# A graph network's edge loop: w1 rows asked for earlier, three smaller last node blocks, and fewer groups copied by hand

## The chip, the cores and the metric

The kernel runs on one core of a Trainium2 chip. The core has five engines that run their own queues of instructions in order: TensorE (PE; its weight loads are shown as PEld), VectorE (DVE), ScalarE (ACT), GpSimd (POOL) and SyncE (SP, which here only issues transfers). The metric is the device time of one execution in microseconds; of several timed runs the median counts.

## What is computed

One layer of a gated graph network over 12500 nodes and 400000 edges, everything in float32. Edges are sorted by their destination `dst`; the source `src` of an edge is any node. With `h = relu(layernorm(x))`:

```python
h = jnp.concatenate([x[s], x[d], ea], axis=-1)          # x is h here; 128 + 128 + 32 columns
m = jax.nn.relu(h @ w1 + b1) @ w2 + b2
agg = jax.ops.segment_sum(m, d, num_segments=x.shape[0])
gi = agg @ w_ih + b_ih
gh = x @ w_hh + b_hh
...
r = jax.nn.sigmoid(i_r + h_r)
z = jax.nn.sigmoid(i_z + h_z)
n = jnp.tanh(i_n + r * h_n)
return (1.0 - z) * n + z * x
```

The result is added to the layer's input. The last four lines are the node update; what stands above `gi` is the edge work.

## The kernel before

**Tables first.** A short first stage normalises all nodes, keeps `h` transposed in the core's memory (`hT_all`, 128 features by 12500 nodes) and writes the table A = h @ w1[0:128] to main memory. A second table, B = h @ w1[128:256] + b1, is made in batches of 512 nodes during the edge loop (`batch_product`, `batch_store`, 32 groups ahead of their use, AHEAD). So the first product of an edge is A[src] + B[dst] + ea @ w1[256:288].

**Groups and units.** The edges come in 391 groups of 1024 (8 tiles of 128 edges), each group in two units of four tiles, 782 units in all. Since edges are sorted by destination, a group touches few nodes: two windows of 32 rows of B, eight nodes apart, hold all destinations of a group.

**One unit.** `stages(u)` writes down work for several units ahead, and `other(phase)` sprinkles the rest between. For a unit:
- `fetch(q)` loads tile L for two groups: destinations repeated over 64 partitions (L533) and the transposed edge features (L536), two transfers of 256 KB on SP's queue. L has three buffers, so the load of L number q waits until TensorE has read number q - 3.
- `onehot_T` on VectorE turns the destinations in L into a one-hot matrix (L545).
- `window_rows(k)` loads the B rows of the group's two windows into RW, beside the w1 rows of the edge features (L575, two transfers of 16 KB). RW has four buffers, taken in turn by k mod 4. Since B lives in main memory, the load waits for the store of its batch.
- `pre(u)` on TensorE multiplies L by RW (L644): this gives B[dst] + ea @ w1 for the unit's four tiles in one bank.
- The A[src] part comes in one of two ways. For most groups, `gather(k)` has POOL issue eight indirect transfers, one for each tile of 128 rows of A (L152), into G, a ring of 12 buffers; VectorE adds G to the product and applies the relu in one instruction (`add`, L668). For "hand groups" nothing is gathered: ScalarE or VectorE copies the 1024 needed columns of `hT_all` one by one (`one_by_one`; ScalarE one column at a time, L905; VectorE two at a time, L912, unpacked by L917), TensorE multiplies them by w1 (L655), and ScalarE applies the relu (`relu`, L675). SPREAD says how many hand groups each engine has; `run_jobs` spreads the copying of one evenly over the units since the one before. The last hand groups are 382 (VectorE) and 385 (ScalarE).
- `seg(u)` on TensorE sums the edges' rows onto the windows' 64 places with another one-hot matrix (L683, L688), and `take(k)` copies the sums out after each group (L696).

The first ten groups are gathered from x itself and normalised in place, since A is not ready by then.

**Order.** Every engine runs its queue as the program writes it. `gathers(u)` writes the gathers of a group down as soon as the buffer's last reader has been written; POOL's queue holds nearly nothing else, so it runs ahead until a buffer is missing. SP's queue holds all loads and stores, `fetch`, `window_rows`, the stores of B and of the output, and stands still at the first one that must wait. `window_rows(k + 3)` is written in the second unit of group k, in phase 2; `pre` of group k's first unit is written three units before it, in `stages`.

**Nodes.** Nodes are updated in blocks of up to 14 groups (512 nodes). BLOCKS lists each block's first group, its groups and its width. When the loop reaches the next block's first group, `node(b)` starts: it sums the block's windows (`sum_of`, L713), carries the overlap over (`carry`, L724, L727), makes the four gates on TensorE, applies sigmoid and tanh on ScalarE, combines on VectorE and stores the rows. It yields some 13 times, and one step is taken at the end of each unit. LEAST bounds the distance of two blocks' first nodes; NW counts the blocks of full width. ROOM enters a check that no window needs rows of B that are not stored yet; if a check of that kind fails, a slow general path recomputes all, which did not run here.

**The last block** has a function of its own, `last_node`, whose steps are taken in the units LAST_STEPS. Its eight groups' sums are added one by one as they come, and its gates start before the last sum is there. Two of its steps, the gate matmuls (L830, L833), are taken after the loop, between the last `seg` and the last `take`'s `sum_of`.

Of the kernel before, what the change touches and what calls it, by code (L numbers as in the profile page):

```python
# [9 lines left out]
F32 = mybir.dt.float32  # L10
# [17 lines left out]
NU = 2 * NP  # L28

V = 32  # L30
# [2 lines left out]

BP, BW = 14, 512
DMIN = 320
BLOCKS = [(BP * b, BP, BW) for b in range(27)] + [(378, 5, 256), (383, 8, 320)]
NB = len(BLOCKS)
NW = 27
LEAST = [DMIN] * 28 + [16]
QP = 2  # L40
W = 96
NT = -(-N // 128)
# [3 lines left out]
GBUFS = 12  # L46
BATCH = 512
AHEAD = 32
ROOM = V * (AHEAD - 2)
PLACE = 20  # L50
CH = PLACE * PAIR
LOAD = {"act": 16, "dve": 32}
PIECE = 128
STEP = {"act": 4, "dve": 8}
SPREAD = {"dve": 26, "act": 24}
START = {"dve": 16, "act": 4}
NR = 12672

# [4 lines left out]
def tile_gnn(ctx: ExitStack, tc: tile.TileContext, x, src, srcT, dstT, dstP, eaT, eaP, w1, b1, w2T, b2,  # L63
# [11 lines left out]
    ps2 = ctx.enter_context(tc.tile_pool(name="ps2", bufs=2, space=bass.MemoryType.PSUM))  # L75
# [662 lines left out]
    def node(b):  # L738
        w = BLOCKS[b][2]
        g0, xb, offs = block_start(b)  # L740
        pt = ps1.tile([128, 512], F32, name="nd")[:, :w]
        pd = ps1.tile([128, 512], F32, name="misc")[:, :w]
        nc.vector.tensor_copy(dcol[:2 * V, :len(offs)], sums[:, :len(offs), D])
        zero(pt)
        for i in range(len(offs)):
            sum_of(b, pt, offs, i)
        zero(pd)
        for i in range(len(offs)):
            degree_of(b, pd, offs, i)
        d = step_of(b)  # L750
        yield 1
        carry(b, TOT, pt, d)
        carry(b, DEG[0:1, :], pd[0:1, :], d)
        yield 1
        g = nc.tensor.value_load(blk_i[0:1, b:b + 1], min_val=0, max_val=N - w)
        hT = hT_all[:, bass.ds(g, w)]

        def gate(name, i, with_h, with_s):
            c = slice(i * D, (i + 1) * D)
            ci = slice(2 * D, 3 * D) if i == 3 else c  # L760
            pg = ps1.tile([128, 512], F32, name=name)[:, :w]
            nc.tensor.matmul(pg, brow[:, c], DEG[:, :w], start=True, stop=False)  # L762
            if with_h:
                nc.tensor.matmul(pg, whh_s[:, ci], hT, start=False, stop=not with_s)
            if with_s:
                nc.tensor.matmul(pg, w2ih[:, ci], TOT[:, :w], start=False, stop=True)  # L766
            return pg

        pr = gate("nd", 0, True, True)
        yield 1  # L770
        r = temp(w)
        nc.scalar.activation(r, pr, AF.Sigmoid)  # L772
        ph = gate("misc", 3, True, False)
        yield 1
        t = temp(w)
        nc.vector.tensor_tensor(t, r, ph, op=ALU.mult)
        pi = gate("nd", 2, False, True)
        yield 1
        nc.vector.tensor_tensor(t, t, pi, op=ALU.add)
        pz = gate("misc", 1, True, True)  # L780
        yield 1
        nc.scalar.activation(t, t, AF.Tanh)
        z = temp(w)
        nc.scalar.activation(z, pz, AF.Sigmoid)
        yield 1
        gv = nc.vector.value_load(blk_i[0:1, b:b + 1], min_val=0, max_val=N - w)
        q = r
        nc.vector.tensor_tensor(q, hT_all[:, bass.ds(gv, w)], t, op=ALU.subtract)
        yield 1
        nc.vector.tensor_tensor(q, q, z, op=ALU.mult)  # L790
        yield 1
        nc.vector.tensor_tensor(q, q, t, op=ALU.add)
        yield 1
        po = ps1.tile([128, 512], F32, name="nd")[:w // 4, :]
        for i in range(4):
            nc.tensor.transpose(po[:, i * D:(i + 1) * D], q[:, i::4], ident)
        yield 1
        nc.vector.tensor_tensor(xb, xb, po.rearrange("p (i f) -> p i f", i=4), op=ALU.add)
        yield 4 if b < NW - 1 else 1
        nc.sync.dma_start(out[bass.ds(g0, w), :].rearrange("(p i) f -> p i f", i=4), xb)  # L800

    def last_node():
        b = NB - 1
        k0, n, w = BLOCKS[b]
        g0, xb, offs = block_start(b)
        yield
        pd = wide[1][:, :w]
        zero(pd)
        for i in range(n):
            degree_of(b, pd, offs, i)  # L810
        d = step_of(b)
        g = nc.tensor.value_load(blk_i[0:1, b:b + 1], min_val=0, max_val=N - w)
        hT = hT_all[:, bass.ds(g, w)]
        gv = nc.vector.value_load(blk_i[0:1, b:b + 1], min_val=0, max_val=N - w)
        h = hT_all[:, bass.ds(gv, w)]
        pt = wide[0][:, :w]
        zero(pt)
        for i in range(n - 4):
            sum_of(b, pt, offs, i)
        yield  # L820
        carry(b, DEG[0:1, :], pd[0:1, :], d)
        for i in range(n - 4, n - 1):
            yield
            sum_of(b, pt, offs, i)
        yield

        def gate(pool, name, i, h_too):
            c = slice(i * D, (i + 1) * D)
            pg = pool.tile([128, 512], F32, name=name)[:, :w]
            nc.tensor.matmul(pg, brow[:, c], DEG[:, :w], start=True, stop=False)  # L830
            if h_too:
                ci = slice(2 * D, 3 * D) if i == 3 else c
                nc.tensor.matmul(pg, whh_s[:, ci], hT, start=False, stop=i == 3)  # L833
            return pg

        def finish(pg, i):
            nc.tensor.matmul(pg, w2ih[:, i * D:(i + 1) * D], TOT[:, :w], start=False, stop=True)

        pr = gate(ps1, "nd", 0, True)
        ph = gate(ps1, "misc", 3, True)  # L840
        yield
        pi = gate(ps2, "seg", 2, False)
        pz = gate(ps2, "pre", 1, True)
        yield
        sum_of(b, pt, offs, n - 1)
        carry(b, TOT, pt, d)
        finish(pr, 0)
        finish(pi, 2)
        finish(pz, 1)
        r, t, z = temp(w), temp(w), temp(w)  # L850
        nc.scalar.activation(r, pr, AF.Sigmoid)
        nc.vector.tensor_tensor(t, r, ph, op=ALU.mult)
        nc.vector.tensor_tensor(t, t, pi, op=ALU.add)
        nc.scalar.activation(z, pz, AF.Sigmoid)
        nc.scalar.activation(t, t, AF.Tanh)
        nc.scalar.activation(r, pz, AF.Sigmoid, scale=-1.0)
        nc.vector.tensor_tensor(z, z, h, op=ALU.mult)
        nc.vector.tensor_tensor(t, t, r, op=ALU.mult)  # L858
        nc.vector.tensor_tensor(t, t, z, op=ALU.add)  # L859
        po = ps1.tile([128, 512], F32, name="nd")[:w // 4, :]  # L860
        for i in range(4):
            nc.tensor.transpose(po[:, i * D:(i + 1) * D], t[:, i::4], ident)  # L862
        nc.vector.tensor_tensor(xb, xb, po.rearrange("p (i f) -> p i f", i=4), op=ALU.add)  # L863
        nc.sync.dma_start(out[bass.ds(g0, w), :].rearrange("(p i) f -> p i f", i=4), xb)
# [93 lines left out]
    gathers(0)  # L958
    for q in range(3):
        fetch(q)  # L960
    for k in range(3):
        window_rows(k)


# [30 lines left out]
                    left.pop(0)  # L995

    last = last_node()
    LAST_STEPS = (NU - 8, NU - 6, NU - 5, NU - 4, NU - 2, NU - 1)

    for u in range(NU):  # L1000
        k, h = divmod(u, 2)
        gathers(u)
        if h == 0:
            if k % QP == 0:
                fetch(k // QP + 3)
            if k and k == BLOCKS[block(k)][0]:
                nodes_left.append([node(block(k) - 1), 2 if k < BLOCKS[-1][0] else 1])
            if k % PLACE == 1:
                indices(k // PLACE + 2)
            if k % PLACE == 5:  # L1010
                place(k // PLACE + 1)
                dst_tile(k // PLACE + 2)
            if k == NP - 20:
                check_windows()
        if u == min(START.values()) - 2:
            nc.vector.tensor_scalar(at[:NJ, :], at[:NJ, :], 4.0, float(H_AT), op0=ALU.mult, op1=ALU.add)

        def other(phase):
            run_jobs(u, phase)
            if h == 0 and phase == 1 and batch_due(k):  # L1020
                batch_product(batch_due(k), wide[1], p3, "xb", 2)
            if h == 1 and phase == 1 and batch_due(k):
                batch_store(batch_due(k))
            if h == 1 and phase == 2:
                window_rows(k + 3)
            if h == 0 and phase == 3:
                take(k - 1)
            if phase == 3:
                step(nodes_left)
                if u in LAST_STEPS:  # L1030
                    next(last)

        other(0)
        stages(u)
        other(1)
        other(2)
        seg(u)
        if u == 0:
            node_setup()
        other(3)  # L1040
    for it, _ in nodes_left:
        run(it)
    next(last)
    next(last)
    take(NP - 1)
    run(last)

# [168 lines left out]
```

## Time and profile before

| | before |
|---|---|
| median of 3 timed runs | 3548.33 us (3529.08 to 3559.73) |
| the profiled execution, whole | 3567.68 us |
| its span, first to last instruction | 3565.9 us |
| granted clock of TensorE in it, mean | 0.783 |
| matmuls for RW by L (L644) | 3128, of 495 ns, busy 1149.9 us |
| segment sums (L688) | 6250, of 319 ns, busy 592.3 us |
| matmuls of hand groups (L655) | 416 of VectorE's groups, 384 of ScalarE's |
| transfers on POOL's queue | 178.76 MB, 21.5% of 16 engines' span |
| transfers on SP's queue | 153.56 MB, 15.8% |

A row of the profile's costliest groups gives line, engine, operation, tiles written and read, shapes and count, then the engine's busy time in it and the mean duration of one in ns, then the time the engine sat idle just before them and what ended most of that. Instructions of one engine overlap, so count times mean can be more than the busy time. A row of the waits says who waited for whom: microseconds in total, how many times, and the longest. "Issue" is time in which an engine waited for nothing that the profile shows. A row of the timeline begins with its start and length in us. SP's rows there are the issue of a transfer, not the transfer.

### The profile page before, as it was taken

The page shows a single profiled execution, that of the slowest core. Times are in us where ns is not written, and L with a number is a line of the kernel's source. Part 1 is how long each engine was busy: PE and PEld are TensorE (multiplying, and loading weights), DVE is VectorE, ACT ScalarE, POOL GpSimd, SP SyncE. Part 2 cuts the span into 40 slices and gives each one's busy share as a digit, 9 for nine tenths or more (in the row PEclk, how much of TensorE's full clock was granted, in tenths as well). Part 3 has the DMA queues.
Part 4 walks back from the last instruction along what each step waited for, and adds up shares of the span by engine and source line. Part 5 has one row for each costly group of instructions (what it writes and reads, how often), then busy time and mean ns, then how long its engine had stood idle before and what let it go on. Part 6 is the DMA issues. An engine that isn't in the chain of part 4 may idle for free. (4 is left out here: it accounts for less than half of the span.)

```text
span 3565.9 us, 80442 instructions
## 1 busy us (share of the span) xinstructions
PE 2409.1 (68%) x13224; PEld 1536.2 (43%) x13224; DVE 2266.0 (64%) x16484; ACT 2661.4 (75%) x25007; POOL 2614.4 (73%) x2734
## 2 busy tenths in 40 slices
PE   6567666675776676577667766765766676667768
PEld 6444444443444444344444443443444344434435
DVE  7656666666656666666566666666666666666664
ACT  5497778768777778787678688768876887796782
POOL 7677777777777777777777777777777777777770
PEclk8788877777777877777777878778777788787868
DMA  6433333333333333333333333333333333333431
GB/s 198 100 87 93 93 94 93 90 96 93 92 89 93 92 92 95 93 96 92 94 94 96 92 95 95 93 93 96 95 91 95 94 98 96 96 91 91 95 94 31
DMA packets 188489, 337.57 MB, mean 95 GB/s; under 512 B 65118, under 2 KB 108701, under 8 KB 187967
## 3 DMA queue, kind: packets, MB, share of 16 engines
q0 software_dynamic: 87200, 178.76, 21.5%
q1 hardware_dynamic: 100623, 153.56, 15.8%
q14 instruction: 412, 3.38, 0.3%
q8 instruction: 110, 1.80, 0.2%
q10 hardware_dynamic: 144, 0.07, 0.0%
HBM read 311.87 MB, written 20.27 MB: 93 GB/s over the span
## 5 line engine op out<-in xcount | busy, mean ns | idle before, releaser
L152 POOL DMA_INDIRECT G<-A,src_i x2648 | 2540.1, 959 | 839.6 <-issue 761.9
L905 ACT COPY HE_act<-hT_all 128x4 uint8 x24576 | 2470.3, 189 | 57.9 <-issue 38.3
L644 PE MATMUL pre<-RW,L 128*128 128x256 f32 x3128 | 1149.9, 495 | 1079.9 <-DMA RW<-B 827.5
L912 DVE SCALAR_TENSOR_TENSOR both<-hT_all 128x4 uint16 x13312 | 1138.0, 153 | 970.6 <-issue 961.4
L644 PEld LDWEIGHTS pre<-RW,L 128*128 128x128 f32 x3128 | 672.9, 240 | 1379.5 <-issue 669.8
L688 PE MATMUL seg<-RB,OH 128*32 128x129 f32 x6250 | 592.3, 319 | 0.0
L668 DVE CUSTOM_DVE_ANT_0 RB<-pre,G 128x512 f32<-128x512 f32 x662 | 448.5, 677 | 133.3 <-PE pre L644 98.8
L675 ACT ACTIVATE RB<-pre 128x512 f32<-128x512 f32 x120 | 70.7, 589 | 481.6 <-PE pre L655 481.3
L688 PEld LDWEIGHTS seg<-RB,OH 128*32 128x32 f32 x6250 | 326.8, 123 | 208.5 <-issue 159.0
L545 DVE TENSOR_SCALAR L<-L,node_of 64x512 f32<-64x512 int32 x383 | 187.2, 489 | 6.1 <-DMA L<-in_dstP 5.9
L772 ACT ACTIVATE gt<-nd 128x512 f32<-128x512 f32 (+1 forms) x28 | 16.5, 588 | 228.8 <-PE nd L766 228.8
L596 DVE TENSOR_TENSOR OH<-dloc,wide 128x256 f32<-128x256 f16 (+1 forms) x392 | 158.9, 406 | 0.5 <-issue 0.3
L696 DVE COPY sums<-seg 64x129 f32<-64x129 f32 x391 | 108.1, 277 | 17.2 <-PE seg L688 17.2
L683 PEld LDWEIGHTS <-zrow 1*64 1x64 bf16 x391 | 41.4, 106 | 143.4 <-issue 134.8
L683 PE MATMUL seg<-zrow 1*64 1x129 bf16 x391 | 99.4, 254 | 2.3 <-DVE sums L696 2.2
L917 DVE COPY HE_dve<-both 128x512 uint8<-128x512 uint8 x208 | 93.2, 448 | 7.1
L713 PE MATMUL nd<-spot,sums 64*128 64x40 f32 x766 | 94.2, 285 | 0.0
L713 PEld LDWEIGHTS nd<-spot,sums 64*128 64x128 f32 x766 | 90.7, 193 | 6.2 <-issue 6.1
L152 POOL DMA_INDIRECT G<-in_x,src_i x77 | 72.8, 945 | 24.4 <-issue 23.2
L655 PEld LDWEIGHTS pre<-w1a,HE_dve 128*128 128x128 f32 x416 | 75.6, 226 | 9.1
L655 PEld LDWEIGHTS pre<-w1a,HE_act 128*128 128x128 f32 x384 | 73.7, 239 | 9.1
L762 PE MATMUL nd<-DEG,brow 34*128 34x512 f32 (+1 forms) x112 | 75.0, 755 | 0.9 <-DVE DEG L727 0.9
(193 smaller groups left out, 1414.3 us busy)
## 6 DMA issues: line engine op xcount, KB each, us to landing
L<-in_dstP SPq DMA_DIRECT2D x195, 256.0 KB
L<-in_eaP SPq DMA_DIRECT2D x195, 256.0 KB
G<-A,src_i POOLq DMA_INDIRECT x2648
RW<-B SPq DMA_DIRECT2D x782, 16.0 KB
xb<-in_x SPq DMA_DIRECT2D x27, 256.0 KB
out<-xb SPq DMA_DIRECT2D x27, 256.0 KB
xs<-in_x SPq DMA_DIRECT2D x11, 512.0 KB
A<-asb SPq DMA_DIRECT2D x11, 512.0 KB
```

Of the source, the lines that this page charges most:

```text
L152: nc.gpsimd.indirect_dma_start(out=G[k][:, j, a, :], out_offset=None, in_=table, in_offset=bass.IndirectOffsetOnAxis(ap=src_i[c][:, i:i + ...
L545: nc.vector.tensor_scalar(o, i, node_of[:, k:k + 1], None, op0=ALU.is_equal)
L596: nc.vector.tensor_tensor(o, d.to_broadcast(shape), i.to_broadcast(shape), op=ALU.is_equal)
L644: nc.tensor.matmul(PP[u][:, 2 * i:2 * i + 2, :], Ls[k // QP][:, c0:c0 + 128], RW[k % 4], start=True, stop=not raw)
L655: nc.tensor.matmul(PP[u][:, 2 * i + a, :], cols, w1a, start=False, stop=n + 1 == len(l) or l[n + 1][1] != j)
L668: nc.vector._custom_dve(TENSOR_ADD_SAT, out=RB[u % 4][:, :, :D], in0=PP.pop(u), in1=unit(u), s0=float("inf"), s1=0.0)
L683: nc.tensor.matmul(SEG[k][:2 * V, :D + 1], zrow[:, :2 * V], zrow[:, :D + 1], start=True, stop=False)
L688: nc.tensor.matmul(SEG[k][V * a:V * (a + 1), :D + 1], OH[k][:, j, a, :], RB[u % 4][:, (j % 2) * 2 + a, :D + 1], start=False, stop=all(b != ...
L696: nc.vector.tensor_copy(sums[:, slot(block(k), k - BLOCKS[block(k)][0]), :], pm[:2 * V, :D + 1])
L713: nc.tensor.matmul(p[:, bass.ds(offs[i], V + SHIFT)], sums[:, slot(b, i), :D], spot, start=False, stop=i == len(offs) - 1)
L905: nc.scalar.copy(he[:, e * 4:e * 4 + 4], column(v))
L912: nc.vector.scalar_tensor_tensor(both[:, (e0 % PIECE + i) // 2, :], column(vals[i + 1]), 256.0, column(vals[i]), op0=ALU.mult, op1=ALU.add)
```

## The change

`window_rows` is asked for group k + 4 at the start of group k's first unit, ahead of that unit's `fetch`, and no more for k + 3 in the second unit. Four groups are asked for ahead of the loop. ROOM goes down to fit. SPREAD takes VectorE from 26 hand groups to 25 and ScalarE from 24 to 15. The last three node blocks are 10, 9 and 8 groups (before: 14, 5 and 8, behind one full block more), and `last_node` makes three of its gates in units of the loop, one each, with a step in unit NU - 3 that was not there; the z gate goes into the bank that held the degrees. After the loop `take` follows at once.

```diff
-BLOCKS = [(BP * b, BP, BW) for b in range(27)] + [(378, 5, 256), (383, 8, 320)]
+BLOCKS = [(BP * b, BP, BW) for b in range(26)] + [(364, 10, 384), (374, 9, 352), (383, 8, 320)]
-NW = 27
-LEAST = [DMIN] * 28 + [16]
+NW = 26
+LEAST = [DMIN] * 27 + [256, 128]
...
-ROOM = V * (AHEAD - 2)
+ROOM = V * (AHEAD - 4)
...
-SPREAD = {"dve": 26, "act": 24}
+SPREAD = {"dve": 25, "act": 15}
...
-        yield 4 if b < NW - 1 else 1
+        yield 4 if b < NW else 1
...
         carry(b, DEG[0:1, :], pd[0:1, :], d)
-        for i in range(n - 4, n - 1):
-            yield
-            sum_of(b, pt, offs, i)
         yield
...
-        pr = gate(ps1, "nd", 0, True)
-        ph = gate(ps1, "misc", 3, True)
+        sum_of(b, pt, offs, n - 4)
+        pz = gate(pd, 1, True)
         yield
-        pi = gate(ps2, "seg", 2, False)
-        pz = gate(ps2, "pre", 1, True)
+        pr = gate(bank(ps1, "nd"), 0, True)
+        yield
+        sum_of(b, pt, offs, n - 3)
+        ph = gate(bank(ps1, "misc"), 3, True)
+        yield
+        sum_of(b, pt, offs, n - 2)
+        pi = gate(bank(ps2, "pre"), 2, False)
         yield
         sum_of(b, pt, offs, n - 1)
...
-    for k in range(3):
+    for k in range(4):
         window_rows(k)
...
-    LAST_STEPS = (NU - 8, NU - 6, NU - 5, NU - 4, NU - 2, NU - 1)
+    LAST_STEPS = (NU - 8, NU - 6, NU - 5, NU - 4, NU - 3, NU - 2, NU - 1)
...
         if h == 0:
+            window_rows(k + 4)
             if k % QP == 0:
                 fetch(k // QP + 3)
...
-            if h == 1 and phase == 2:
-                window_rows(k + 3)
...
-    next(last)
-    next(last)
     take(NP - 1)
     run(last)
```

More of the change, by code (lines that the diff above doesn't have):

```diff
@@ L821, in last_node, with gate @@
         carry(b, DEG[0:1, :], pd[0:1, :], d)
-        for i in range(n - 4, n - 1):
-            yield
-            sum_of(b, pt, offs, i)
         yield
-        def gate(pool, name, i, h_too):
+        def gate(pg, i, h_too):
             c = slice(i * D, (i + 1) * D)
-            pg = pool.tile([128, 512], F32, name=name)[:, :w]
             nc.tensor.matmul(pg, brow[:, c], DEG[:, :w], start=True, stop=False)
@@ L834, in gate, with bank @@
             return pg
+        def bank(pool, name):
+            return pool.tile([128, 512], F32, name=name)[:, :w]
         def finish(pg, i):
             nc.tensor.matmul(pg, w2ih[:, i * D:(i + 1) * D], TOT[:, :w], start=False, stop=True)
-        pr = gate(ps1, "nd", 0, True)
-        ph = gate(ps1, "misc", 3, True)
+        sum_of(b, pt, offs, n - 4)
+        pz = gate(pd, 1, True)
         yield
-        pi = gate(ps2, "seg", 2, False)
-        pz = gate(ps2, "pre", 1, True)
+        pr = gate(bank(ps1, "nd"), 0, True)
[5 more added lines that the diff above has]
+        pi = gate(bank(ps2, "pre"), 2, False)
         yield
```

## The prediction

> **What bounds the kernel now.** I read the page first, then the waits of each engine, then stretches of the timeline. The first and second parts and the costliest groups:
>
> ```profile
> PE 2409.1 (68%) x13224; PEld 1536.2 (43%) x13224; DVE 2266.0 (64%) x16484; ACT 2661.4 (75%) x25007; POOL 2614.4 (73%) x2734
> ...
> POOL 7677777777777777777777777777777777777770
> ...
> L152 POOL DMA_INDIRECT G<-A,src_i x2648 | 2540.1, 959 | 839.6 <-issue 761.9
> L905 ACT COPY HE_act<-hT_all 128x4 uint8 x24576 | 2470.3, 189 | 57.9 <-issue 38.3
> L644 PE MATMUL pre<-RW,L 128*128 128x256 f32 x3128 | 1149.9, 495 | 1079.9 <-DMA RW<-B 827.5
> ...
> L152 POOL DMA_INDIRECT G<-in_x,src_i x77 | 72.8, 945 | 24.4 <-issue 23.2
> ```
>
> No engine is full by its share. The waits (who waited for what: us in total, times, longest) say more:
>
> ```profile
> PE pre L644 <- DMA RW<-B: 827.5, 162, 10.1
> POOL G L152 <- issue: 785.1, 2576, 0.3
> ...
> ACT RB L675 <- PE pre L655: 481.3, 56, 28.3
> ...
> POOL G L152 <- DVE RB L668: 27.9, 25, 4.8
> ...
> DVE RB L668 <- DMA G<-A,src_i: 3.0, 1, 3.0
> ```
>
> Two things run nearly in step. TensorE waits 162 times, 5.1 us each (827.5/162), for the rows RW: about once for two groups. POOL pauses 0.305 us (785.1/2576) before almost every gather, never longer than 0.3 by "issue"; so a gather takes 0.959 + 0.305 = 1.264 us of POOL's queue and the queue is full, though the page shows it 73% busy. Busy time by stretch (length, POOL busy, its gathers) says the same:
>
> ```profile
> 1181.00:3479.00 2298.00, 1744.26 (x1816) 0.78 0.38 94
> ```
>
> 2298.00/1816 = 1.2654 us a gather for 2.3 ms on end. For a buffer POOL waited only 27.9 us in all; 25 x 0.3 of it is the usual pause, so 20.4 us. The readers of G waited for a gather once, 3.0 us. So the edge loop sets the end by its own pace, with POOL's queue right beside it: 2725 gathers now end at 3479.1 us, and the loop runs some 10 groups behind them.
>
> The timeline shows why RW is late:
>
> ```profile
> 2009.97 0.57 SPq L533 DMA_DIRECT2D L<-in_dstP  x1
> 2010.59 0.50 SPq L536 DMA_DIRECT2D L<-in_eaP  x1
> 2011.20 0.99 SPq L575 DMA_DIRECT2D RW<-B  x2
> ...
> 2021.20 1.29 PE L644 MATMUL pre<-RW,L 128*128 128x256 f32 x3 [2.44 <-DMA RW<-B]
> ```
>
> SP issues the two 256 KB loads of L, then the RW rows behind them; they are used 10.0 us later, after a wait. The end:
>
> ```profile
> 3478.20 0.94 POOL L152 DMA_INDIRECT G<-A,src_i  x1 [0.30 <-issue]
> ...
> 3544.72 0.69 DVE L668 CUSTOM_DVE_ANT_0 RB<-pre,G 128x512 f32<-128x512 f32 x1 [0.41 <-PE pre L644]
> ...
> 3548.72 0.78 PE L830 MATMUL nd<-DEG,brow 34*128 34x320 f32 x2
> ...
> 3553.65 0.41 PE L713 MATMUL wide<-spot,sums 64*128 64x40 f32 x2
> ...
> 3559.93 0.68 DVE L863 TENSOR_TENSOR xb<-xb,nd 80x512 f32<-80x512 f32 x1 [0.83 <-PE nd L862]
> ```
>
> The last gather is issued 66 us before the loop adds its rows; from that add to the end of the span (3565.9) are 21.2 us, 4.9 of them gate matmuls (3548.7 to 3553.6) between the last segment sum and the last window sum.
>
> **Rows asked for earlier.** window_rows moves from unit 2k'-5 to the start of 2k'-8 for group k', ahead of fetch in SP's order. By SP's order the rows behind a fetch are then those used seven units on (five by the program, two more since SP runs ahead to its next wait). A unit lasts (3544.7 - 138.1)/780 = 4.37 us from first to last add, so 7 units are 30 us against the 11 us needed. The 827.5 us go; kept at the other bound (all of it stays) they cost nothing new. The buffer k' mod 4 was last read in unit 2k'-10, so the earlier request waits for nobody. Moved with it: 391 x 2 DMAs of 0.334 us on SP and the wait for the stores of B (213.0 us in 23 times, 9.3 each). Behind that wait on SP now stands the fetch of two units later, whose data is due six units after it: 26 us cover 9.3 us. Nothing. The loop alone would come to about 3566 - 828 = 2738 us.
>
> **Hand groups.** Ten groups fewer are copied column by column. ScalarE loses 9 x 1024 copies at 2470.3/24576 = 0.1005 us: 926 us. But it was waiting for TensorE already (481.3 us), so that is worth nothing by itself. VectorE loses 512 x 1138.0/13312 = 44 us and gains 20 adds of 0.677 = 14 us; TensorE loses 80 matmuls of 0.275 = 22 us; none of these is late. POOL gains 10 x 8 = 80 gathers in a queue that has no gap: 80 x 1.2654 = 101.2 us, all on the path. Bounds of the pace: the 77 first gathers, with no copying beside them, took 945 + 305 = 1.250 us (2728 gathers after the first 77 x 0.0154 = 42 us less); the ring waits of 20.4 us stay (20 us more). I take 1.2654, from the longest stretch with the same neighbours.
>
> **Last blocks and early gates.** Still 29 blocks and 391 window sums; the columns are 26 x 512 + 384 + 352 + 320 = 14368 against 14400. Worth nothing while TensorE waits for gathers; uncovered, the 10-group block's sums would cost 28 x 0.118 = 3.3 us on it (28 took 3.31 us). In the tail three of the four gates move into loop units where TensorE waits. One of 0.8 us stays: 4.9 - 0.8 = 4.1 us saved. Another 2.5 us go: the last segment sum began 3547.92, 2.5 us after the add ended, behind matmuls that will be done by then. So 21.2 - 6.6 = 14.6 us from add to end, plus landing: the last gather packet ended 3480.45, 1.3 us behind POOL, and say 0.6 us of semaphores (an estimate from the 0.3 pauses): 16.5 us.
>
> **Sum.** With the RW wait gone the loop needs 2 x 4.37 - 827.5/391 = 6.6 us a group, POOL 8 x 1.2654 = 10.1 us a gathered one; the loop catches up, the 10-group lead is used up, and POOL sets the end: 3479.1 - 20.4 + 101.2 = 3559.9, + 16.5 = 3576.4 us span, + 1.8 around it (3567.68 - 3565.9) = 3578 us, 0.3% above the profiled run. That run lies 0.55% over the median 3548. If timed runs are as much quicker, 3559; if POOL's pace is the same in each, 3578. I take 3566, +0.5%: the large gain is paid back by the gathers.
>
> **The skill against this.** The Trainium skill's page "Perfetto Trace Analysis", section "Identifying the Most-Contended Engine", tells to go by occupancy, for GpSimd and ScalarE too, and to relieve the fullest first. Here that is ScalarE (75%), and the change takes a third of its work; POOL at 73% would have room for 80 gathers. The same page, "DMA Instruction — SWDGE (GPSIMD)", leaves waiting and dispatch of such a DMA outside the profiled window, which would make the 0.3 us part of a gather's price; the constant pause agrees.
>
> **Rivals.**
> (1) Quicker gathers. In the loop's trace, gathers with no ScalarE copy beside them took 952 ns and the others 961, and a third of the copies goes; timed runs have no profiler. At 1.250 us: 3578 - 42 = 3536, with the 0.55% off 3517. For it: the 945 row. Against: only 77 gathers, and 24 groups of copying become 15, not none.
> (2) Slower: the lag is not used up at the end. The last hand groups, 382 and 385, lie in the last nine, and two node blocks fall into the last 34 units. While the loop does them POOL runs on, and what lag is left at the last gather adds to the end one for one. Before, it was 3543.1 - 3479.1 = 64 us (start of the last group's first add). From group 386 on five gathered groups win back 5 x (10.1 - 6.6) = 17.5 us. A lag of 38 us there leaves 20: 3598 us, or 3586 on the way to the median. It decides by 1% from 6 us left (unscaled) to 18 (on 3566). Against: 3.5 us are won at each gathered group all the way.
> (3) The pause is not POOL's own, and a hungry loop closes it: 101 + 10 us of first waits + 2728 x 0.959 + 16.5 = 2744 us, like the loop's own 2738. For it: the shares. Against: 2576 pauses all of 0.3, also with full index tiles and free buffers. The occupancy rule of the Trainium skill's page above goes the way of this rival.
> (4) The rows are still late, since L's loads go ahead of some of them: the loop keeps 4.37 us a unit, ends near 3566, POOL's queue behind it at 3578: no change in sign or size.
>
> **How the numbers follow.** A measurement of this kernel tells about 1% from no change: below 3513 faster, above 3584 slower. POOL's queue at its pace: 0.50 (0.40 within, 0.06 slower, 0.04 faster), own range 3545 to 3584. Rival 1: 0.20 (0.12 faster, 0.08 within). Rival 2: 0.19 (0.18 slower, 0.01 within). Rival 3: 0.07, faster. Rival 4: 0.04, within. Faster 0.23, within 0.53, slower 0.24. The range takes rival 1 with its discount and some run-to-run spread (3529 to 3560 before) and rival 2's 3598: 3495 to 3605; outside are rival 3 and the ends of 1 and 2.
>
> **What would show it.** TensorE's wait for RW near nothing; VectorE's adds waiting for G, some 300 times, several hundred us in all; 2805 gathers still at 1.25 to 1.27 us with no ring wait; the last gather ending near 3560 and the span 15 to 18 us later; ScalarE near 1735 us busy. Wrong would be: gather starts under 1.2 us apart (rival 3), a last add more than 10 us after the last gather (rival 2), RW waits of hundreds of us (rival 4).

## The result, and the profile after

The changed kernel takes 3582.26 us (median of 18 runs, 3573.55 to 3588.86) against 3559.64 us for the kernel before (18 runs, 3527.78 to 3574.95): ratio 1.0078, 95% interval 1.0055 to 1.0100. It is slower by less than one per cent. The forecast of 3566 had the sign and the order of size; 3578, the sum without the discount, was closer. The runs lie three times closer together than before (15 us against 47). The profile shown below is of the fastest of them, 3573.55 us.

Two of the three series of experiments met a condition in which the kernel before took 5351 and 5357 us instead of 3554 (the second series' chip bears the same number as the first's), so every run is compared with the kernel before of its own series alone.

The page of the changed kernel, its engines, POOL's busy tenths over time, and the groups that answer to those shown of before:

```profile
PE 2510.3 (70%) x13064; PEld 1584.3 (44%) x13064; DVE 2233.1 (63%) x15993; ACT 1728.3 (48%) x15771; POOL 2692.7 (75%) x2814
...
POOL 7777777777777777777777777777777777777776
...
L152 POOL DMA_INDIRECT G<-A,src_i x2728 | 2618.3, 960 | 837.6 <-issue 776.7
L644 PE MATMUL pre<-RW,L 128*128 128x256 f32 x3128 | 1192.6, 512 | 898.7 <-DVE RB L668 874.0
...
L909 ACT COPY HE_act<-hT_all 128x4 uint8 x15360 | 1543.0, 189 | 47.1 <-issue 34.5
...
L668 DVE CUSTOM_DVE_ANT_0 RB<-pre,G 128x512 f32<-128x512 f32 x682 | 463.2, 679 | 303.9 <-DMA G<-A,src_i 260.7
```

ScalarE lost 933 us of work and the kernel did not gain a microsecond. TensorE still waits 898.7 us ahead of L644 (1079.9 before), but for another thing: not for RW but for VectorE's add (L668), which in turn waits 260.7 us for the gathered rows G. POOL has work to the very end now: the last of its 40 slices, 0 before, is 6. Its share is 75% (73% before), and still it is the full queue, as a long stretch and its own waits show (length, POOL's busy time and gathers; then who waited for what, us, times, longest):

```profile
1181.00:3479.00 2298.00, 1744.26 (x1818) 0.75 0.37 92
```

```profile
POOL G L152 <- issue: 799.9, 2625, 0.3
...
POOL G L152 <- DVE RB L668: 7.0, 23, 0.3
```

1818 gathers in 2298 us, two more than before: 1.264 us each. What is left of waiting for a buffer (7.0 us in 23 times) is 0.3 us a time, the usual pause, so nothing. The end in the timeline (start, length):

```profile
3554.63 0.94 POOL L152 DMA_INDIRECT G<-A,src_i  x1 [0.30 <-DMA G<-A,src_i]
...
3557.31 0.69 DVE L668 CUSTOM_DVE_ANT_0 RB<-pre,G 128x512 f32<-128x512 f32 x1 [4.16 <-DMA G<-A,src_i]
...
3558.86 0.78 PE L826 MATMUL pre<-DEG,brow 34*128 34x320 f32 x2
...
3559.49 0.31 PE L713 MATMUL wide<-spot,sums 64*128 64x40 f32 x2
...
3566.08 0.68 DVE L867 TENSOR_TENSOR xb<-xb,nd 80x512 f32<-80x512 f32 x1 [1.24 <-PE nd L866]
```

The last gather ends at 3555.6, the last add starts 1.7 us later, after 4.16 us of waiting for it, and the span ends at 3571.5. Before, 66 us lay between gather and add. One gate is left behind the last segment sum.

### The profile page after: what moved, and what is told of

The parts are those of the page before. It is cut to its first block, busy times and chain, and to the rows that moved or that the text cites. A ratio compares the mean times of both kernels' runs of the same rounds, so it can differ in the third digit from the quotient of the medians.

```text
span 3571.5 us, 70126 instructions
## 1 busy us (share of the span) xinstructions
PE 2510.3 (70%) x13064; PEld 1584.3 (44%) x13064; DVE 2233.1 (63%) x15993; ACT 1728.3 (48%) x15771; POOL 2692.7 (75%) x2814
## 5 line engine op out<-in xcount | busy, mean ns | idle before, releaser
L152 POOL DMA_INDIRECT G<-A,src_i x2728 | 2618.3, 960 | 837.6 <-issue 776.7
L644 PE MATMUL pre<-RW,L 128*128 128x256 f32 x3128 | 1192.6, 512 | 898.7 <-DVE RB L668 874.0
L916 DVE SCALAR_TENSOR_TENSOR both<-hT_all 128x4 uint16 x12800 | 1100.8, 155 | 938.6 <-issue 930.5
L909 ACT COPY HE_act<-hT_all 128x4 uint8 x15360 | 1543.0, 189 | 47.1 <-issue 34.5
L644 PEld LDWEIGHTS pre<-RW,L 128*128 128x128 f32 x3128 | 692.5, 246 | 1231.7 <-DVE RB L668 988.1
L668 DVE CUSTOM_DVE_ANT_0 RB<-pre,G 128x512 f32<-128x512 f32 x682 | 463.2, 679 | 303.9 <-DMA G<-A,src_i 260.7
L688 PE MATMUL seg<-RB,OH 128*32 128x129 f32 x6250 | 627.4, 334 | 1.7 <-DVE RB L668 1.4
L772 ACT ACTIVATE gt<-nd 128x512 f32<-128x512 f32 (+2 forms) x28 | 16.5, 589 | 541.6 <-PE nd L766 541.6
L713 PEld LDWEIGHTS nd<-spot,sums 64*128 64x128 f32 x766 | 122.1, 250 | 8.7 <-issue 8.7
L713 PE MATMUL nd<-spot,sums 64*128 64x40 f32 x766 | 126.0, 339 | 0.0
L782 ACT ACTIVATE gt<-gt 128x512 f32<-128x512 f32 (+2 forms) x28 | 17.4, 621 | 150.3 <-DVE gt L779 150.3
L655 PE MATMUL pre<-w1a,HE_dve 128*128 128x128 f32 x400 | 73.6, 316 | 0.0
```

The source lines that it names most:

```text
L152: nc.gpsimd.indirect_dma_start(out=G[k][:, j, a, :], out_offset=None, in_=table, in_offset=bass.IndirectOffsetOnAxis(ap=src_i[c][:, i:i + ...
L644: nc.tensor.matmul(PP[u][:, 2 * i:2 * i + 2, :], Ls[k // QP][:, c0:c0 + 128], RW[k % 4], start=True, stop=not raw)
L655: nc.tensor.matmul(PP[u][:, 2 * i + a, :], cols, w1a, start=False, stop=n + 1 == len(l) or l[n + 1][1] != j)
L668: nc.vector._custom_dve(TENSOR_ADD_SAT, out=RB[u % 4][:, :, :D], in0=PP.pop(u), in1=unit(u), s0=float("inf"), s1=0.0)
L688: nc.tensor.matmul(SEG[k][V * a:V * (a + 1), :D + 1], OH[k][:, j, a, :], RB[u % 4][:, (j % 2) * 2 + a, :D + 1], start=False, stop=all(b != ...
L713: nc.tensor.matmul(p[:, bass.ds(offs[i], V + SHIFT)], sums[:, slot(b, i), :D], spot, start=False, stop=i == len(offs) - 1)
```

## The experiments

Theory Q: POOL's queue sets the end wherever the loop is quicker than it; each gathered group costs 10.1 us. Theory V: VectorE's column copies are the next limit and the rows are worth little. Theory I came up in the first series: the issue of the column copies sets the pace, and the number of groups by hand decides.

### First series: one part each, in the condition of 5351 us

**e1: the early rows alone**, on the kernel before (the lines that move the request; ROOM and the four groups ahead of the loop go with them).

```diff
...
+            window_rows(k + 4)
             if k % QP == 0:
                 fetch(k // QP + 3)
...
-            if h == 1 and phase == 2:
-                window_rows(k + 3)
```

> The kernel before with the early rows alone (groups by hand 26 and 24, old blocks and old tail). Theory Q (POOL's queue sets the end once the rows are early): ten groups fewer than the changed kernel to gather, 80 x 1.2654 = 101 us off its 3582, and the old tail some 5 us on: about 3486 us, 2% under the kernel before; VectorE waits for G, the last add within 5 us of the last gather. Theory V (VectorE is the next limit, busy 2266 us and 961 us idle between its column copies in the kernel before): no less than about 3540 us, and VectorE does not wait for G.

**e2: the hand groups alone**, on the kernel before.

```diff
-SPREAD = {"dve": 26, "act": 24}
+SPREAD = {"dve": 25, "act": 15}
```

> The kernel before with 25 and 15 groups by hand, rows and tail as before. Theory Q: POOL's queue ends near 3560 in the trace, the loop keeps its RW waits of some 800 us and about 4.4 us a unit, so it arrives nearly with POOL: 3580 to 3600 us, 0.5 to 1% over the kernel before. Theory V: fewer copies free the loop, so it is quicker than before, below 3550 us.

**e3: the changed kernel, rows as before** (the diff of e1 undone).

> The changed kernel with the rows asked for as before (second unit of the group, three groups ahead). Theory Q: the early rows buy nothing while 2805 gathers fill POOL's queue: within 0.5% of the changed kernel, 3575 to 3600 us, although TensorE waits some 800 us for RW again. Theory V: the rows matter whatever the gathers do: over 3620 us.

**e4: the changed kernel, groups as before** (the diff of e2 undone).

> The changed kernel with 26 and 24 groups by hand (early rows, new blocks and new tail kept). Theory Q: 3582 - 101 = 3481 us, some 2.2% under the kernel before, ScalarE back at 2660 us busy and not late. Theory V: as before the change, 3540 us or more, with VectorE not waiting for G.

| | median, us | against before (5350.59) | 95% interval |
|---|---|---|---|
| e1, rows alone | 5331.49 | 0.9962 | 0.9935 to 0.9988 |
| e2, groups alone | 5048.11 | 0.9431 | 0.9379 to 0.9483 |
| e3, changed, rows as before | 5030.25 | 0.9386 | 0.9331 to 0.9441 |
| e4, changed, groups as before | 5334.28 | 0.9971 | 0.9944 to 0.9998 |

None of the expected times was met, since all assumed the usual condition. The waits of e1 show what was different:

```profile
ACT HE_act L905 <- issue: 2092.5, 3144, 2.1
DVE both L912 <- issue: 1654.6, 1791, 2.5
POOL G L152 <- DVE RB L668: 1617.9, 191, 36.6
```

In the kernel before's own trace, in the usual condition, ScalarE stood 38.3 us, 95 times, ahead of its copies with no cause shown, VectorE 961.4 us, 839 times. Here it is 2092.5 us in 3144 times and 1654.6 us in 1791, in the midst of the copies: one wait to eight copies on the average. They come in bursts. ScalarE's timeline shows a stretch of 20 us in which the copies start 0.71 us or twice that apart, singly or a few at a time, and then 30 of them in 3 us:

```profile
399.58 0.19 ACT L905 COPY HE_act<-hT_all 128x4 uint8 x1 [0.52 <-issue]
400.30 0.19 ACT L905 COPY HE_act<-hT_all 128x4 uint8 x1 [0.52 <-issue]
...
417.11 3.02 ACT L905 COPY HE_act<-hT_all 128x4 uint8 x30 [0.23 <-issue]
```

A gather and a DMA packet take what they took (956 ns a gather; the 4096-byte packets of POOL's queue 262 ns in the mean, before 272). POOL is not the bound here at all: it waited 1617.9 us for buffers. ScalarE was busy 2930.9 us and stood at least 2092.5 for nothing shown, together 94% of the span of 5326.8. So with 24 groups the engine that copies is nearly full. Taking nine groups off ScalarE and one off VectorE (e2, e3) gives 6%, while the early rows bring 0.4% (e1) and, with the new tail, 0.3% (e4). With 15 groups ScalarE is no longer full (e2: busy 1944.0 us, standing 1738.0, 73% of 5042.5), and what sets the pace then is not shown. Fewer groups by hand pay in this condition and cost in the usual one. The changed kernel as a whole was not run in it. What slows the issue in this condition isn't told by any trace here.

### Second series: the usual condition

**f1: the changed kernel again.**

> The changed kernel itself, beside the kernel before on the same chip. On a chip where the kernel before takes some 3560 us: 3582 us, ratio 1.008, by theory Q. On the chip of the runs before, where it took 5351 us and ScalarE and VectorE stood 2092 and 1655 us for nothing that the profile shows: near the two kernels with 25 and 15 groups there, 5030 to 5050 us, ratio 0.94; theory I (issue): what bounds there is the issue of the column copies, so that the count of groups by hand decides and the early rows do nothing.

**f2: the early rows alone**, the kernel of e1.

> The kernel before with the early rows alone. On a chip of 3560 us: theory Q 3486 us (101 us less than the changed kernel for 80 gathers, 5 us more for the old tail), VectorE waiting for G at the end; theory V (VectorE next in line) 3540 us or more. On the chip of 5351 us: 5331 us again.

**f3: more groups by hand**, on the changed kernel.

```diff
-SPREAD = {"dve": 25, "act": 15}
+SPREAD = {"dve": 26, "act": 28}
```

> The changed kernel with 26 groups by VectorE and 28 by ScalarE, 14 groups fewer gathered than in the changed kernel. On a chip of 3560 us, theory Q: 3582 - 14 x 10.1 = 3440 us, if ScalarE's 28 x 103 + 190 = 3070 us busy still fit; theory V: 3540 us or more. On the chip of 5351 us, theory I: four groups more than 24, at some 30 us each (5331 less 5030 for ten), so about 5450 us.

**f4: fewer groups by hand**, on the changed kernel.

```diff
-SPREAD = {"dve": 25, "act": 15}
+SPREAD = {"dve": 25, "act": 5}
```

> The changed kernel with only 5 groups by ScalarE, 25 by VectorE. On a chip of 3560 us, theory Q: ten groups more to gather, 3582 + 101 = 3683 us; theory V: no slower than the changed kernel. On the chip of 5351 us, theory I: ten groups fewer to copy at 30 us each, about 4740 us.

| | gathers | last gather ends, us | median, us | against before (3553.5) | 95% interval |
|---|---|---|---|---|---|
| f4, 25 and 5 | 2885 | 3657.0 | 3680.83 | 1.0368 | 1.0319 to 1.0418 |
| f1, 25 and 15 | 2805 | 3556.7 | 3580.88 | 1.0084 | 1.0049 to 1.0120 |
| f2, 26 and 24, old tail | 2725 | 3461.2 | 3493.02 | 0.9842 | 0.9796 to 0.9887 |
| f3, 26 and 28 | 2693 | 3431.4 | 3450.99 | 0.9718 | 0.9674 to 0.9762 |

This is theory Q. Ten groups less by hand cost 3680.83 - 3580.88 = 100 us, 1.25 us a gather (101 expected). Fourteen more bring 129.9 us, 9.3 us a group (10.1 expected); part of the rest is that the gathers are a little longer there (962 ns against 959) and that POOL meets a wait for a buffer again. The early rows alone make the kernel before 60 us quicker (3493 us, 3486 expected), and the other parts then give back 87.9 us. The waits of VectorE's adds for gathered rows, first f4, then f1, f2 and f3:

```profile
DVE RB L668 <- DMA G<-A,src_i: 351.0, 114, 8.2
```

```profile
DVE RB L668 <- DMA G<-A,src_i: 270.4, 89, 6.5
```

```profile
DVE RB L668 <- DMA G<-A,src_i: 126.5, 44, 6.4
```

```profile
DVE RB L668 <- DMA G<-A,src_i: 70.0, 23, 6.4
...
POOL G L152 <- DVE RB L668: 13.8, 26, 5.0
```

The more is gathered, the longer the loop stands for gathers; in f3 only 70 us are left, and POOL has a wait of 5.0 us for a buffer again. So theory V is wrong as to its number (3540 us) but right that a limit of the loop lies not far below: 3449.4 - 70.0 = 3379 us is an estimate of where the loop of f3 would end by itself. Whether VectorE is that limit is not shown: in f3 it was busy 2253.1 us and stood 942.6 us ahead of its copies, 93% of the span, but ScalarE was busy 3073.2 us, 89%. f3 is the quickest version that was run here, 2.8% under the kernel before.

### Third series: 5357 us for the kernel before again

**g1 and g2: e3 and e2 once more**, meant for the usual condition.

> The changed kernel with the rows asked for as in the kernel before, again, where the kernel before takes some 3555 us. Theory Q (POOL's queue of 2805 gathers sets the end, the loop is quicker than it either way: 4.37 us a unit with the RW waits against 4.54 us that POOL needs): 3575 to 3600 us, within 0.5% of the changed kernel's 3581, with RW waits of several hundred us back and fewer waits for G. Theory V (the rows matter whatever the gathers do): over 3620 us. If the kernel before takes 5350 us again: 5030.

> The kernel before with 25 and 15 groups by hand, again. Theory Q: POOL's queue ends near 3560, the old tail and what is left of the loop's lag behind it: 3585 to 3600 us, ratio 1.008 to 1.013. Theory V (fewer copies free the loop): below 3540 us. If the kernel before takes 5350 us again: 5050.

**g3: still more by hand** (the diff of f3 with 30 in place of 28).

> The changed kernel with 26 groups by VectorE and 30 by ScalarE, two more than in the run of 28. Theory Q: 3451 less 2 x 10 = 3431 us, ScalarE near 3280 us busy. Against it, theory S (ScalarE becomes the bound, since a group by hand takes it 103 us of the 112 us that 30 groups leave): no quicker than 3445 us, and VectorE or TensorE waits for ScalarE while POOL waits for buffers. If the kernel before takes 5350 us: about 5500.

**g4: the changed kernel with the old last blocks and the old last_node.**

```diff
-BLOCKS = [(BP * b, BP, BW) for b in range(26)] + [(364, 10, 384), (374, 9, 352), (383, 8, 320)]
+BLOCKS = [(BP * b, BP, BW) for b in range(27)] + [(378, 5, 256), (383, 8, 320)]
...
-        sum_of(b, pt, offs, n - 4)
-        pz = gate(pd, 1, True)
+        pr = gate(ps1, "nd", 0, True)
+        ph = gate(ps1, "misc", 3, True)
...
```

> The changed kernel with the old last blocks and the old last_node (early rows and 25 and 15 groups kept). If the tail is what the sum says, 6.6 us: 3581 + 6 = 3587 us, its last add to the end of the span some 6 us longer. Rival: the gates' place is worth nothing, 3581, since what ends the tail is the chain of gates after the last sum. If the kernel before takes 5350 us: no difference that can be told.

Against 5356.55: g1 5121.32 (ratio 0.9546, 0.9517 to 0.9574), g2 5121.34 (0.9554, 0.9528 to 0.9579), g3 5908.11 (1.1034, 1.1014 to 1.1054), g4 5110.36 (0.9520, 0.9492 to 0.9547). The three with 25 and 15 groups can't be told apart, so neither rows nor tail show in this condition (from the last add to the end g4, with the old tail, takes 21.0 us and g1, with the new one, 19.9), and their questions stay unanswered for the usual one. g3 has the sign that theory I gives, but not the size (5500 us expected, 5908 measured):

```profile
ACT HE_act L909 <- issue: 2102.5, 3145, 2.0
...
POOL G L152 <- DVE RB L668: 2169.5, 197, 44.1
```

ScalarE, busy 3553.1 us and standing 2102.5 us, fills 96% of a span of 5901.8, and POOL waits 2169.5 us for buffers. The expectation took 30 us a group from the step between 15 and 24 groups, where ScalarE is not full all the way. Over 24 each costs some 92 us (5908.11 less 5356.55, over six), near the 103 us that a group's copies keep ScalarE busy (3370.1 us in g3 less 2749.3 in e1, over six). The standing time does not grow in step with the copies (1738.0 us at 15 groups in e2, 2092.5 at 24 in e1, 2102.5 here), so it isn't a price of each copy; what it is stays open. The answer to theory S in the usual condition is open too: 28 groups are the most that were run there. By these numbers a kernel for both conditions would hardly take f3's counts, though f3 itself was not run in this one.

## Why the prediction was right, and where its steps were off

**RW waits.** The 827.5 us went, as the step says: 874.0 of TensorE's 898.7 us are put down to VectorE's add, and a single wait of 7.9 us for RW is left:

```profile
L644 PE MATMUL pre<-RW,L 128*128 128x256 f32 x3128 | 1192.6, 512 | 898.7 <-DVE RB L668 874.0 <-ACT RB L675 9.8 <-DMA RW<-B 7.9
```

That this is worth nothing by itself in the changed kernel was reasoned from the queue and is not shown: the run that was to show it in the usual condition (g1) met the other one. What is shown is the other half: with the 2725 gathers of before, the early rows are worth 60 us (f2), down to the end of POOL's queue and no further.

**Gathers.** 80 x 1.2654 = 101.2 us on the path: f4 against f1 measures 100. The last gather was put at 3559.9 and ended at 3555.6 and 3556.7 in the two profiles. This term carries the result, and it is right in mechanism and in size.

**The loop catches up.** Right in kind, mis-sized: that the loop needs 6.6 us a group took all of the RW wait off and put nothing in its place. In the changed kernel's trace POOL's lead is used up only some 93 groups on: the first add that waits for a gather starts at 881.6 us, 748 us after the loop's first relu at 133.3, so 8.0 us a group. VectorE's waits from 860 to 3556 us:

```profile
DVE both L916 <- issue: 734.5, 638, 2.5
DVE RB L668 <- DMA G<-A,src_i: 256.6, 85, 8.0
```

All its 260.7 us for gathers lie behind 860 us, these 85 waits and that of the last add, where "some 300" were expected, and beside them three times as much standing ahead of the column copies: there VectorE loads its registers with the numbers of the columns (800 loads of 32 numbers, 2.16 us each, and 816 waits ahead of the copies in the whole run). The prediction counted 44 us for a VectorE group's copies by busy time alone, and left this idle time out. That it is what makes 8.0 us out of 6.6 is argued, not shown by a run: VectorE's busy 2233.1 us, the 930.5 us of standing and the 260.7 us for gathers fill 96% of the span. It did not matter for the end here, since 8.0 is under the 9.1 us a group that POOL needs on the average of all groups (3555.6 / 391). It matters more for f3, whose loop is nearly at its own pace.

**The tail.** 16.5 us from the last gather's end to the end of the span; measured 15.9, and 22.8 in the second profile of the same kernel, f1. The difference of 6.9 us goes with TensorE's clock (last section), which the prediction took as that of the kernel before. So the near hit of the first profile is partly luck; f3 and f4, with the same tail, took 18.1 and 22.1 us.

**The discount.** The step that was off: "If timed runs are as much quicker, 3559; if POOL's pace is the same in each, 3578. I take 3566". The runs are not quicker: 18 of them have a median of 3582. The kernel before spreads over 47 us and its profiled execution, 3567.68 us, was a longer one than most; the changed kernel, which ends with POOL's queue of equal gathers, spreads over 15. That the loop's pace is what varies is likely by this, but not shown. The middle was a hedge between two cases, and the constant pause in the profile spoke for the second.

**The rivals.** (1) Quicker gathers: 960 ns in the mean where 959 were before, although a third of ScalarE's copies is gone, and 960 in f4 with 5 groups; wrong. (2) A lag left at the end: last add 1.7 us after the last gather; wrong here. (3) The pause closed by a hungry loop: 2625 pauses, still 0.3 us; wrong. The Trainium skill's page "Perfetto Trace Analysis", section "Identifying the Most-Contended Engine", would have relieved ScalarE: in f4 a relief of ten groups more cost 100 us, in f3 13 groups put back onto ScalarE and one onto VectorE brought 130. In the condition of 5351 us the same rule points the right way: ScalarE's 55% is the highest share there too, and e2 gained 6%. Share of busy time did not tell the two cases apart; standing ahead of the next instruction, engine by engine, did. (4) Rows still late: wrong.

## What to carry to other kernels

Take a queue's price per item from start to start over a long stretch, pause and all, and ask whether any pause is ever longer than the rest: an engine at 73% whose gaps were all equal was full here. When two chains run in step, speeding up one moves the end only as far as the other, and a second edit in the same change that loads that other one takes the gain back; price the edits against the chain that is left. A count of hand-made work that balances engines holds for one condition of issue only, so measure it where the kernel will run.

## What the runs showed of the hardware

TensorE's granted clock in the tail differs from run to run, also of one program. The last stretch of the kernel before (a backlog of matmuls up to the end), of the changed kernel's first profile, and of f1, f2 and f3, where the loop stood for gathers (stretch, length, busy time of PE, PEld, DVE, ACT and POOL, then the clock):

```profile
3544.00:3566.00 22.00, 12.58 (x74) 7.09 (x72) 6.36 (x14) 1.67 (x4) 0.00 (x0) 0.89 0.06 15
```

```profile
3557.00:3571.00 14.00, 5.35 (x26) 3.08 (x26) 4.99 (x12) 1.67 (x4) 0.00 (x0) 0.78 0.06 15
```

```profile
3557.00:3579.00 22.00, 13.90 (x43) 7.15 (x42) 4.99 (x12) 1.56 (x4) 0.00 (x0) 0.58 0.04 12
```

```profile
3462.00:3489.00 27.00, 16.96 (x42) 8.47 (x42) 5.97 (x13) 1.56 (x4) 0.00 (x0) 0.56 0.05 13
```

```profile
3433.00:3449.00 16.00, 7.77 (x24) 4.59 (x24) 4.99 (x12) 1.56 (x4) 0.00 (x0) 0.50 0.04 11
```

From the last add to the end are 14.2 us in the first profile of the changed kernel and 21.1 in f1, the same program: one gate's pair of matmuls (L829) took 0.81 us in the one and 1.43 in the other. The mean clock of the tail alone does not tell its length: f3 has the lowest, 0.50, and takes 16.4 us. By these traces it counts when the clock falls. In f3 it was 1.00 up to 3433 us, where the last add starts, and in the first profile back at 1.00 from 3551 us, 6 us ahead of it. In f1 it was 0.50 from 3540 us on, 18 us ahead of the last add, so the gates written ahead of the last segment sum were late and that sum began 5.3 us after the add's start, 0.75 us in the first profile. TensorE was hardly idle in that stretch of f1 (stretch, length, PE's busy time, clock):

```profile
3540.00:3548.00 8.00, 8.00 (x41) 0.50 0.21 57
...
3556.00:3564.00 8.00, 8.00 (x31) 0.50 0.06 16
```

With the old tail it was 21.1 us before and 26.7 in f2. The early gates are worth some 6 us where the clocks of the tail are alike (26.7 in f2 at 0.56 against 21.1 in f1 and 20.4 in f4, both at 0.58), near the 6.6 of the sum. The Trainium skill's page "TensorE: Matmul & The Clock Gate", Part 1, lets the clock follow how busy TensorE has just been, at half rate by default and at full rate after about 3.4 us of sustained work. The half rate agrees with the 0.50; the 24 us at 0.50 in f1 from 3540 to 3564, with TensorE busy 23.5 of them, do not agree with so early a rise. What held the clock down there is not shown.

The second thing is the condition in which ScalarE and VectorE stand, in bursts, ahead of one in eight of many small instructions: the kernel before takes 5351 us there, 1.5 times the usual, with gathers, DMA packets, single copies (190 ns on ScalarE in e1, 189 in the kernel before) and the loads of their column numbers (1.03 us on ScalarE in both) as long as ever. TensorE's granted clock is lower too, 0.67 in the mean against 0.78; whether that is a cause or comes of the waiting is not shown. The cause of the condition is not shown either.
